# Where raw weights lie, when x is asked for, and how far up the queue a chunk's load stands: three edits at the seam between two layers of a four-layer kernel

## The chip, the cores and the metric

The kernel runs on one core of a Trainium2 chip. A core has five engines that run side by side, each its own list of instructions in order: TensorE (PE) multiplies matrices, VectorE (DVE) and ScalarE (ACT) work element by element, GpSimd (POOL) does too, and SyncE (SP) issues transfers between the chip's memory and the on-chip buffer (SBUF), which 16 DMA engines carry out. The metric is the device time of one execution in microseconds (us), as the median of several runs.

## The reference

The input is `x`, 8 images of 96 channels and 64 x 64 pixels. Four layers follow one another; each adds its result to `x`, and each normalises its input over groups of three channels of one image first:

```
x = x + L0(gn(x))   # a selective state-space scan along all 4096 pixels of an image
x = x + L1(gn(x))   # real FFT -> gated channel mixing -> inverse FFT -> 1x1 projection
                    # -> batch norm over all 8 images -> gelu
x = x + L2(gn(x))   # 3x3 convolution -> offsets -> bilinear sampling -> patches of 4 x 4 pixels
                    # -> four scans (two orders, each forward and backward) -> layer norm -> gate
x = x + L3(gn(x))   # deformable 3x3 convolution
```

Two facts matter here. The batch norm of L1 takes its mean and variance over all eight images, so no image of L1 can be finished until the last has been transformed. And L2 works on chunks of 512 pixels (8 rows of an image), each of which needs normalised `x` with one row above and one below.

## The kernel before

Layer 0 and layer 2, and layer 3 too, are written out by hand as a list of slots: for every slot and engine a list of small functions, issued in that order (`Plan`, `Slots`, and `sl.at(slot, queue, function)`). "sp" stands for the queue of transfers. Layer 1 (the Fourier layer) is written in order of its loops. What is not under such an order is placed by the framework's scheduler, which fills each engine's list by its own estimate of when things are ready.

**Layer 1** goes through the images one after the other: `load` (both halves of `xh`), `down` (L808, into `tr`), `along` (L833, reads `tr`), `gate`, `project`, `back`, `up`, and `store` (L930 to L932), which writes the image `y` to memory in two transfers and reads it back in another layout as `yr`. A tile pool `l1y` has four buffers for `yr`, so the last four images (4 to 7) are still on chip at the end; `kept` holds them. Then come the batch norm's constants (L975 to L983). Then `between()` is called, which for this program is `weights2`: the weights of layer 2. Then the last step of layer 1 for the four kept images (L984 to L997): load `x`, `gelu` of `yb` in place, `x + y`, store, and the statistics that layer 2 needs. The other four images (0 to 3) are finished inside layer 2's slots, in 16 pieces of 96 x 1024 elements (`piece`, L1003 to L1020 and L1653 to L1679): five pieces are asked for in slot -92, five in slot -60, six in slot -46, each piece two loads, and each is stored one slot after its add.

**`weights2`** (L1029) loads raw weights and folds them into the form that layer 2 uses. The folded ones live in a pool `l2c` on the right side of SBUF, that is, at its upper end, and stay for all of layer 2. The raw ones (`l2_wx`, `l2_off1`, `l2_xp`, `l2_dt`, `ds` and small ones) live in a pool `l2t`, which is closed when the folding is done. It takes the default side, the left, directly above `yr`.

**Layer 2** has 64 chunks. Chunk `i` has its base at slot `B = 48 i`; one slot holds one group of scans: a load `dd<-delta` (L319), two exponentials on ACT (L327), a product on POOL (L348), two scans and two products on DVE (L1501, L358), two matmuls. Ahead of the scans of a chunk goes `front` (L1176): `load` of `xl` in slot B - 92 (L1185), `normal` in slot B - 89 (L1190, on ACT, into `pad`), the convolution (L1213) from slot B - 86, offsets, and sampling on POOL up to slot B - 46. Its last part, a copy on ACT (L1329), is in slot B - 44. For chunk 1, `normal` stands in slot -41, and so follows this copy of chunk 0 in ACT's order. Within a slot the order of a queue is the order of the `sl.at` calls; the pieces are placed before the chunks.

**Pools and waits.** A pool takes a stretch of SBUF. When a stretch is used again by a later pool, the later pool's first accesses must wait for the earlier use. The argument `reuse_waits` says how: with `"pool"`, the default, a new pool waits for everything in the pools that lay there; with `"tile"`, each tile waits only for the tiles whose bytes it takes. In the kernel before every pool has the default. In bytes per partition, the pools that matter are laid out so: `l1c` 17,792 to 23,460; `l1w` to 31,076; `l1y` 31,104 to 96,640; `l1i` (all working tiles of the Fourier passes) 96,640 to 224,128; after it `l2t` 96,640 to 120,736 and, once that is closed, `l1j` (three buffers for `x`) 96,640 to 145,792; `l2f` 17,792 to 126,816 and `l2w` 126,816 to 180,064; `l2c` 183,328 to 229,344.

Of the kernel before, what the change touches and what calls it, by code (L numbers as in the profile page):

```python
# [18 lines left out]
CH = 96  # L19
IH = IW = 64  # L20
NP = IH * IW
# [28 lines left out]
new = Names()  # L50
# [432 lines left out]
def replicate(nc, out, w):  # L483

    p = w.shape[0]
    nc.vector.tensor_copy(
        out.rearrange("p s (r n) -> p s r n", r=GC),
        w.rearrange("p (s n) -> p s n", s=2).unsqueeze(2).to_broadcast([p, 2, GC, HS]),
    )
# [276 lines left out]
def layer1(S, src, mid, dst, st_in, st_out, images, finish, between):  # L766
# [3 lines left out]
    tc, nc = S.tc, S.nc  # L770
    with ExitStack() as ctx:
        cp = ctx.enter_context(tc.tile_pool(name="l1c", bufs=1))
        wp = ctx.enter_context(tc.tile_pool(name="l1w", bufs=2))
# [13 lines left out]
        kept = {}  # L787

        with ctx1:
            ip = ctx1.enter_context(tc.tile_pool(name="l1i", bufs=1))  # L790
# [190 lines left out]
        nc.vector.tensor_tensor(mv[:, 0:1], mv[:, 0:1], vec[:, 0:1], ALU.subtract)  # L981
        nc.vector.tensor_tensor(sc[:, 1:2], mv[:, 0:1], sc[:, 0:1], ALU.mult)
        nc.vector.tensor_tensor(sc[:, 1:2], vec[:, 2:3], sc[:, 1:2], ALU.subtract)  # L983
        between()  # L984
        with ExitStack() as ctx2:
            ip = ctx2.enter_context(tc.tile_pool(name="l1j", bufs=3))
            psp = ctx2.enter_context(tc.tile_pool(name="l1g", bufs=2, space=PSUM))

            here = list(kept)[-4:]
            for b in here:  # L990
                yb = kept[b]
                xb = new(ip, [CH, NP], "x2")
                nc.sync.dma_start(xb, src[b])
                finish.gelu(yb)
                nc.vector.tensor_tensor(xb, xb, yb, ALU.add)
                nc.sync.dma_start(dst[b], xb)
                S.image_stats(st_out[:, b, :], xb, wp, psp, "ps")  # L997
# [30 lines left out]
def weights2(S, cp):  # L1028

    tc, nc = S.tc, S.nc  # L1030
    with tc.tile_pool(name="l2s", bufs=4, space=PSUM) as psa:
        ps_of = lambda: new(psa, [128, NW], "ps_s")

        win = S.load("l2_win", cp)
        off2 = S.load("l2_off2", cp)
        vec = S.load("l2_vec", cp)
        wout = S.load("l2_wout", cp)
        kmean = S.load("k_mean", cp)

        sc = new(cp, [HD, 2], "sc")  # L1040
        sh = new(cp, [HD, 2], "sh")
        S.rsqrt(sc, vec[:, :, 4], cp, "bn")
        nc.vector.tensor_tensor(sc, sc, vec[:, :, 1], ALU.mult)
        nc.vector.tensor_tensor(sh, vec[:, :, 0], vec[:, :, 3], ALU.subtract)
        nc.vector.tensor_tensor(sh, sh, sc, ALU.mult)
        nc.vector.tensor_tensor(sh, sh, vec[:, :, 2], ALU.add)

        wds = new(cp, [CH, DI], "wds")

        wg = new(cp, [HD, 2, CH], "wg")  # L1050
        wb = new(cp, [HD, 2, CH], "wb")
        for h in range(2):
            for t, k in ((wg, 5), (wb, 6)):
                nc.vector.tensor_scalar(
                    t[:, h, :], wout[:, h, :], vec[:, h, k : k + 1], None, ALU.mult
                )

        woff = new(cp, [CH, KT, DI], "woff")  # L1060
        rep_w = new(cp, [CH, 4, 2, 2, 128], "rep_w")
        wd = new(cp, [CH + 1, 4, DI], "wd")
        wuu = new(cp, [CH, 2, DI], "wuu")
        nc.vector.tensor_copy(wuu, win[:, :DI].unsqueeze(1).to_broadcast([CH, 2, DI]))

        centre = new(cp, [HD, 2, HD], "centre")
        nc.vector.tensor_tensor(centre[:, 0, :], S.ident[:HD, :HD], kmean, ALU.subtract)
        nc.vector.tensor_scalar(centre[:, 1, :], kmean, -1.0, None, ALU.mult)
        with tc.tile_pool(name="l2t", bufs=1) as tp:
            wx = S.load("l2_wx", tp)  # L1070
            off1 = S.load("l2_off1", tp).rearrange("e h k o -> e h (k o)")
            xp = S.load("l2_xp", tp)
            dtw = S.load("l2_dt", tp)
            ds = new(tp, [CH, 4, DI], "ds")
            nc.sync.dma_start(ds, S.ins["l2_d"].unsqueeze(0).to_broadcast([CH, 4, DI]))
            nc.vector.tensor_tensor(ds[:, 0:2], ds[:, 0:2], ds[:, 2:4], ALU.add)
            nc.vector.tensor_tensor(wds, ds[:, 0], ds[:, 1], ALU.add)
            nc.vector.tensor_tensor(wds, wds, win[:, :DI], ALU.mult)
            flat = woff.rearrange("c k o -> c (k o)")
            for n in range(4):  # L1080
                at = slice(432 * n, 432 * n + 432)
                ps = ps_of()
                for h in range(2):
                    nc.tensor.matmul(
                        ps[:CH, :432], wx[:, h, :], off1[:, h, at], start=h == 0, stop=h == 1
                    )
                nc.scalar.copy(flat[:, at], ps[:CH, :432])
            xpm = new(tp, [CH, 1, 4 * (RK + 2 * NS)], "xpm")
            ps = ps_of()
            for h in range(2):  # L1090
                nc.tensor.matmul(
                    ps[:CH, : 4 * 38],
                    wx[:, h, :],
                    xp[:, h].rearrange("e k c -> e (k c)"),
                    start=h == 0,
                    stop=h == 1,
                )
            nc.vector.tensor_copy(xpm[:, 0, :], ps[:CH, : 4 * 38])
            for k in range(4):
                at = 38 * k + RK  # L1100
                for what in range(2):
                    replicate(
                        nc, rep_w[:, k, what], xpm[:, 0, at + what * NS : at + (what + 1) * NS]
                    )
                ps = ps_of()
                for h in range(2):
                    nc.tensor.matmul(
                        ps[:RK, :CH], xp[:, h, k, :RK], wx[:, h, :], start=h == 0, stop=h == 1
                    )
                low = new(tp, [RK, CH], f"low{k}")  # L1110
                nc.vector.tensor_copy(low, ps[:RK, :CH])
                ps = ps_of()
                nc.tensor.matmul(ps[:CH, :DI], low, dtw[:RK, k, :], start=True, stop=True)
                m = ORDER.index(k)
                nc.vector.tensor_copy(wd[:CH, m, :], ps[:CH, :DI])
                nc.sync.dma_start(wd[CH : CH + 1, m], S.ins["l2_dt"][RK : RK + 1, k])
        return dict(
            win=win, off2=off2, kmean=kmean, sc=sc, sh=sh, wds=wds, wg=wg, wb=wb, woff=woff,
            rep_w=rep_w, wd=wd, wuu=wuu, centre=centre,
        )  # L1120


def layer2(S, src, dst, st_in, st_out, images, cp, W, ready, finish):


    tc, nc = S.tc, S.nc
    with ExitStack() as ctx:
# [8 lines left out]
            )  # L1136
        )

        fp = ctx.enter_context(tc.tile_pool(name="l2f", bufs=1))
        wp = ctx.enter_context(tc.tile_pool(name="l2w", bufs=1))  # L1140
        sl = Slots(S, cp, wp, psd)
        log_exp_tables(S)
        acol = sl.negative_exp("l2_alog")
# [33 lines left out]
        def front(ch, b, pad, xs, c, B):  # L1177
# [4 lines left out]
            def load():  # L1182
                ch["x"] = new(fp, [CH, 10 * IW], "xl", bufs=2)
                r = 8 * c - 1
                nc.sync.dma_start(  # L1185
                    ch["x"][:, : (hi - lo) * IW], src[b][:, (r + lo) * IW : (r + hi) * IW]
                )
# [11 lines left out]
                r = 0 if c == 0 else 9  # L1199
                nc.gpsimd.memset(pad[:, r, :], 0.0)  # L1200

            sl.at(B - 92, "sp", load)
            sl.at(B - 89, "act", normal)
            if c in (0, NC - 1):
                sl.at(B - 89, "pool", border)
# [102 lines left out]
            def between():  # L1308
                nc.gpsimd.tensor_tensor(ch["bot"], ch["bot"], ch["top"], ALU.subtract)
# [384 lines left out]
        for n, b in enumerate(images):  # L1694
            im = {"bns": new(fp, [CH, NC, 6], f"bns{n % 2}")}
            for c in range(NC):
                i, ch = NC * n + c, {}
                B, pad, xs = PER * i, pads[i % 4], samples[i % 2]
# [388 lines left out]
def program(tc, ins, out, images=range(NB), layers=(0, 1, 2, 3)):  # L2087
    images = list(images)
    with ExitStack() as ctx:
# [9 lines left out]
        def weights():  # L2099
            cp = ctx2.enter_context(tc.tile_pool(name="l2c", bufs=1, side="right"))  # L2100
            held.extend((cp, weights2(S, cp)))

        for n, layer in enumerate(layers):
            to = last if n == len(layers) - 1 else scratch(f"x{layer + 1}_", [CH, NP])
            if n == 0 and layer:
                first_stats(S, x0, st[layer], images)
            if layer == 0:
                layer0(S, x0, to, st[0], st[1], images)
            elif layer == 1:
                mid = scratch("y_", [CH, NP])  # L2110
                finish = Finish(S, x0, mid, to, new(S.pool, [CH, 2], "bn_sc"))
                images, ready = layer1(
                    S, x0, mid, to, st[1], st[2], images, finish, weights if 2 in layers else lambda: 0
                )
            elif layer == 2:
                if not held:
                    weights()
                layer2(
                    S, x0, to, st[2], st[3], images, *held, len(images) if n == 0 else ready, finish
                )  # L2120
                ctx2.close()
            else:
                layer3(S, x0, scratch("t_", [NP - IW, 2, CH]), to, st[3], images)
            x0 = to
# [26 lines left out]
```

## Time and profile before

| what | value |
|---|---|
| time, median of 3 runs | 17438.37 us (17433.97 to 17443.99) |
| the profiled execution | 18287.47 us, its span 18285.7 us |
| DVE busy | 16268.6 us (89% of the span) |
| POOL busy | 15303.1 us (84%) |
| PE busy | 14310.8 us (78%), at a granted clock of 0.900 |
| ACT busy | 10307.5 us (56%) |
| transfers | 2689.99 MB, 147 GB/s over the span |
| layer 1's first load; layer 2's first `xl`; layer 3's first load | at 3021.4, 3803.2 and 14482.5 us |

The profile is one execution, recorded instruction by instruction. "SPq" marks the issue of a transfer on the queue of SP; when its data has landed is read from the waits of those who use it. A line such as "A <- B: 102.6, 2, 75.7" says that A waited for B 102.6 us in all, 2 times, 75.7 us at most. In the chain of waits each line is a start, a length and what ran, and each follows from the one above it.

### The profile page before, as it was taken

The page shows a single profiled execution, that of the slowest core. Times are in us where ns is not written, and L with a number is a line of the kernel's source. Part 1 is how long each engine was busy: PE and PEld are TensorE (multiplying, and loading weights), DVE is VectorE, ACT ScalarE, POOL GpSimd, SP SyncE. Part 2 cuts the span into 40 slices and gives each one's busy share as a digit, 9 for nine tenths or more (in the row PEclk, how much of TensorE's full clock was granted, in tenths as well). Part 3 has the DMA queues.
Part 4 walks back from the last instruction along what each step waited for, and adds up shares of the span by engine and source line. Part 5 has one row for each costly group of instructions (what it writes and reads, how often), then busy time and mean ns, then how long its engine had stood idle before and what let it go on. Part 6 is the DMA issues. An engine that isn't in the chain of part 4 may idle for free.

```text
span 18285.7 us, 141860 instructions
## 1 busy us (share of the span) xinstructions
PE 14310.8 (78%) x34756; PEld 5304.7 (29%) x34756; DVE 16268.6 (89%) x16810; ACT 10307.5 (56%) x17016; POOL 15303.1 (84%) x9100
## 2 busy tenths in 40 slices
PE   8999998858888888898898988889888644434333
PEld 2323334723333333333333333333333211111111
DVE  7999997559999999999999999999999766767667
ACT  6777775546666666766666666676666411111100
POOL 7999995049999999999999999999999656656555
PEclk8999998879999999999999999999999866666666
DMA  7888886269999999999999999999999745444444
GB/s 128 151 153 151 151 151 107 56 139 157 158 158 158 158 158 157 159 157 158 158 157 159 157 159 158 158 158 158 158 157 158 139 127 152 143 136 144 135 129 120
DMA packets 941060, 2689.99 MB, mean 147 GB/s; under 512 B 274482, under 2 KB 276223, under 8 KB 938605
## 3 DMA queue, kind: packets, MB, share of 16 engines
q1 hardware_dynamic: 792781, 2227.79, 70.0%
q0 software_dynamic: 147456, 453.13, 8.4%
q8 instruction: 284, 4.65, 0.1%
q14 instruction: 539, 4.42, 0.1%
HBM read 579.53 MB, written 87.69 MB: 36 GB/s over the span
## 4 chain that ended last, share of the span: by engine, by line
POOL 21%; PE 21%; issue 20%; DVE 18%; another core or an unknown queue 11%; ACT 5%; DMA 4%; SPq 0%; POOLq 0%; DVEq 0%; ACTq 0%
POOL dbu L348 12%; PE ps_y L366 9%; DVE ps_d L1501 7%; DVE dbu L358 6%; DMA dd<-delta 3%; POOL dbu L353 2%; PE ps_k L577 2%; PE ps_a L1820 2%; POOL sp_m L1435 1%; POOL delta L1443 1%; PE ps_o L2054 1%; DVE ps_d L675 1%; POOL sp_w L1438 1%; PE ps_k L1213 1%
## 5 line engine op out<-in xcount | busy, mean ns | idle before, releaser
L348 POOL TENSOR_TENSOR dbu<-dd,brep 128x1024 f32<-128x1024 f32 x3840 | 9062.4, 2376 | 187.8 <-DMA dd<-delta 127.2
L366 PE MATMUL ps_y<-dbu,k_red 128*96 128x512 f32 x15360 | 7447.2, 612 | 817.3 <-DVE dbu L358 496.5
L1501 DVE TENSOR_TENSOR_SCAN ps_d<-ps_d,dbu 128x512 f32<-128x512 f32 x5760 | 6710.3, 1208 | 83.7 <-POOL dbu L348 68.9
L327 ACT ACTIVATE ps_d<-dd,l_alog 128x512 f32<-128x512 f32 x7680 | 4991.7, 681 | 2708.3 <-DVE dbu L358 2571.5
L358 DVE TENSOR_TENSOR dbu<-ps_d,crep 128x512 f32<-128x512 f32 x7040 | 4437.1, 668 | 0.0
L366 PEld LDWEIGHTS ps_y<-dbu,k_red 128*96 128x96 f32 x15360 | 2407.3, 166 | 5459.1 <-issue 3158.6
L1985 POOL DMA_INDIRECT v<-t,idx x2304 | 2185.7, 949 | 1570.1 <-DVE s L2012 730.7
L2012 DVE TENSOR_REDUCE s<-v 128x864 f32<-128x3456 f32 x256 | 1554.2, 6071 | 369.7 <-remote 314.9
L2003 DVE TENSOR_TENSOR v<-v,ps_w 128x3456 f32<-128x3456 f32 x256 | 958.4, 3744 | 735.3 <-ACT ps_w L1995 658.4
L675 DVE TENSOR_TENSOR_SCAN ps_d<-ps_d,carry,dbu 128x512 f32<-128x512 f32 x1120 | 1373.4, 1271 | 80.9 <-POOL dbu L348 50.5
L2031 ACT COPY smp<-ps_t 128x768 f32<-128x768 f32 (+1 forms) x512 | 244.4, 529 | 1793.3 <-remote 1197.4
L1213 PE MATMUL ps_k<-pad,woff 96*96 96x512 f32 x2304 | 1093.8, 597 | 69.4 <-ACT pad L1190 66.9
L1480 PE MATMUL ps_a<-xs,rep_w 96*128 96x512 f32 x2048 | 1097.9, 617 | 53.3 <-ACT brep L1488 51.9
L2023 PE MATMUL ps_t<-k_ident,s 128*128 128x128 f32 (+1 forms) x1792 | 328.3, 334 | 1014.8 <-issue 695.1
L353 POOL TENSOR_TENSOR dbu<-h,crep 128x1024 f32<-128x1024 f32 x320 | 755.7, 2362 | 126.1 <-DVE h L1501 126.1
L1820 PE MATMUL ps_a<-xpad,l_om 96*27 96x512 f32 x1152 | 594.7, 667 | 22.5 <-issue 22.5
L1837 PE MATMUL ps_u<-k_ident,oc 27*128 27x27 f32 x256 | 33.0, 252 | 740.0 <-ACT oc L1832 666.8
L2023 PEld LDWEIGHTS ps_t<-k_ident,s 128*128 128x128 f32 (+1 forms) x1792 | 251.6, 170 | 1149.0 <-issue 985.1
L1213 PEld LDWEIGHTS ps_k<-pad,woff 96*96 96x96 f32 x2304 | 372.1, 164 | 708.9 <-issue 583.1
L1162 POOL MEMSET pad<- 96x660 f32 x4 | 2.4, 648 | 683.1 <-DMA y<-yb 683.1
L1435 POOL TENSOR_TENSOR sp_m<-sp_m,sp_s 128x512 f32<-128x512 f32 x384 | 495.4, 1290 | 59.1 <-ACT sp_s L1423 59.1
L1480 PEld LDWEIGHTS ps_a<-xs,rep_w 96*128 96x128 f32 x2048 | 347.1, 189 | 665.0 <-ACT brep L1488 286.2
(268 smaller groups left out, 17180.5 us busy)
## 6 DMA issues: line engine op xcount, KB each, us to landing
dd<-delta SPq DMA_DIRECT2D x3840, 512.0 KB
v<-t,idx POOLq DMA_INDIRECT x2304
xo<-x SPq DMA_DIRECT2D x128, 192.0 KB
x<-xo SPq DMA_DIRECT2D x128, 192.0 KB
xn<-x SPq DMA_DIRECT2D x64, 192.0 KB
xh<-x SPq DMA_DIRECT2D x16, 768.0 KB
y<-yb SPq DMA_DIRECT2D x16, 768.0 KB
yr<-y SPq DMA_DIRECT2D x8, 1536.0 KB
```

Of the source, the lines that this page charges most:

```text
L327: nc.scalar.activation(da, g.dd[:, 0, :], AF.Exp, scale=g.a[:, i : i + 1])
L348: nc.gpsimd.tensor_tensor(g.dbu, g.dd[:, 1:2, :].to_broadcast([128, 2, NW]), g.b(), ALU.mult)
L353: nc.gpsimd.tensor_tensor(g.dbu, g.both, g.c(), ALU.mult)
L358: nc.vector.tensor_tensor(g.dbu[:, i, :], g.h[i], g.c()[:, i, :], ALU.mult)
L366: self.S.nc.tensor.matmul(y, self.red[:, 80 - GC * g.n : 176 - GC * g.n], g.dbu[:, i, :], start=first and i == 0, stop=last and i == 1,)
L675: nc.vector.tensor_tensor_scan(out, da, dbu, carry[:, n + i : n + i + 1] if c else 0.0, ALU.mult, ALU.add)
L1213: nc.tensor.matmul(ch["pk"][:HD, :], woff[:, k, m * HD : (m + 1) * HD], pad[:, dy : dy + 8, dx : dx + IW], start=k == 0, stop=k == KT - 1,)
L1480: nc.tensor.matmul(dr["pa"], rep_w[:, k, what, s, :], xs[:CH, k % 2, :], start=True, stop=True,)
L1501: nc.vector.tensor_tensor_scan(out[:, way], da[:, way], dbu[:, way], 0.0, ALU.mult, ALU.add)
L1820: nc.tensor.matmul(im["pa"][: 3 * KT, :], om[:, k, :], xpad[:, 8 * c + dy : 8 * c + dy + 8, dx : dx + IW], start=k == 0, stop=k == KT - 1,)
L1985: nc.gpsimd.indirect_dma_start(out=st["v"][:, k].rearrange("p q c -> p (q c)"), out_offset=None, in_=flat, in_offset=bass.IndirectOffsetOn ...
L2012: nc.vector.tensor_reduce(st["s"], st["v"].rearrange("p k q c -> p k c q"), mybir.AxisListType.X, ALU.add,)
```

## The change

There are four edits.

1. The last step of layer 1 opens its pool `l1j` before `between()` instead of after it, issues the loads of `x` of the first three kept images there, and then calls `between()`. Only the fourth image's load stays in the loop. The pool has `reuse_waits="tile"`.
2. The pool `l2t` of the raw weights has `side="right"`: it lies below `l2c`, not above `yr`.
3. The pools `l2f` and `l2w` of layer 2 have `reuse_waits="tile"`.
4. A chunk's load of `xl` stands in slot B - 100 instead of B - 92. `normal` stays in slot B - 89.

```diff
@@ layer1
-        between()
         with ExitStack() as ctx2:
-            ip = ctx2.enter_context(tc.tile_pool(name="l1j", bufs=3))
+            ip = ctx2.enter_context(tc.tile_pool(name="l1j", bufs=3, reuse_waits="tile"))
             psp = ctx2.enter_context(tc.tile_pool(name="l1g", bufs=2, space=PSUM))
 
             here = list(kept)[-4:]
+            x = {}
+
+            def load(b):
+                x[b] = new(ip, [CH, NP], "x2")
+                nc.sync.dma_start(x[b], src[b])
+
+            for b in here[:3]:
+                load(b)
+            between()
             for b in here:
-                yb = kept[b]
-                xb = new(ip, [CH, NP], "x2")
-                nc.sync.dma_start(xb, src[b])
+                if b not in x:
+                    load(b)
+                yb, xb = kept[b], x[b]
                 finish.gelu(yb)
@@ weights2
-        with tc.tile_pool(name="l2t", bufs=1) as tp:
+        with tc.tile_pool(name="l2t", bufs=1, side="right") as tp:
@@ layer2
-        fp = ctx.enter_context(tc.tile_pool(name="l2f", bufs=1))
-        wp = ctx.enter_context(tc.tile_pool(name="l2w", bufs=1))
+        fp = ctx.enter_context(tc.tile_pool(name="l2f", bufs=1, reuse_waits="tile"))
+        wp = ctx.enter_context(tc.tile_pool(name="l2w", bufs=1, reuse_waits="tile"))
@@ front
-            sl.at(B - 92, "sp", load)
+            sl.at(B - 100, "sp", load)
```

## The prediction, made before the kernel was run

> **What bounds the kernel now.** The page comes first: DVE is busy 89% of the span and POOL 84%, but its section of 40 slices shows POOL at 5, 0 and 4 tenths in slices 7 to 9: layer 1, in which POOL has no work, and the seam behind it. The edits act at the seam, so I next cut the time there into stretches. Columns: stretch, its length, then busy time and instructions of each engine, the granted clock, the DMA share, GB/s.
>
> ```profile
> core 0: us, PE busy (x) PEld busy (x) DVE busy (x) ACT busy (x) POOL busy (x), PEclk, DMA share, GB/s
> 3700.00:3746.00 46.00, 14.82 (x44) 6.54 (x44) 14.54 (x51) 18.10 (x10) 5.74 (x9) 0.57 0.61 140
> ...
> 3796.00:3866.00 70.00, 25.97 (x44) 8.39 (x44) 22.98 (x27) 29.86 (x27) 13.21 (x10) 0.62 0.61 161
> 3866.00:3927.00 61.00, 27.68 (x45) 9.24 (x46) 3.51 (x5) 14.23 (x17) 3.27 (x3) 0.64 0.39 95
> ...
> 4100.00:13900.00 9800.00, 8786.98 (x19533) 3096.18 (x19533) 9734.10 (x11247) 6801.38 (x10377) 9592.91 (x5166) 0.99 0.92 158
> ```
>
> From 3700 to 3927 no engine is busy half of the time except DVE in its adds; in the scans after it DVE is busy 99% and POOL 98%. So the seam is bound by latency, and the scans by DVE and POOL. Layer 2 is a fixed order: a seam that ends d earlier ends the kernel d earlier. The chain of waits through the seam:
>
> ```profile
> 3694.17 9.17 DMA y<-yb
> 3703.41 9.23 DMA yr<-y
> 3712.65 7.48 DMA l_xp<-l_xp
> ...
> 3735.81 0.96 PE ps_s L1113 x2
> 3736.79 9.17 DMA x<-x
> ...
> 3746.08 4.43 DVE x L995
> ...
> 3770.36 13.82 DMA x<-x
> ...
> 3788.66 7.05 DMA x<-x
> ...
> 3796.74 6.41 DMA dbu<-y
> ...
> 3803.23 11.77 DMA xl<-x
> ...
> 3815.10 0.88 ACT pad L1190
> ```
>
> `x` is asked for at 3736.79, at once behind the last matmul that reads a raw weight: its buffer is the raw weights' stretch. The pieces' loads wait for the last store of `x` (3788.66 plus 7.05), and chunk 0's `xl` is the eleventh in their queue. Then the timeline of ACT, SP and POOL around chunk 1:
>
> ```profile
> 3864.64 1.11 ACT L1329 COPY xs<-xs 96x512 f32<-96x512 f32 x1 [3.27 <-POOL xs L1316]
> ...
> 3881.31 0.30 SPq L1185 DMA_DIRECT2D xl<-x  x1
> 3892.60 0.92 ACT L1190 ACTIVATE pad<-xl,nm,stats 96x640 f32<-96x640 f32 x1 [26.85 <-DMA xl<-x]
> ...
> 3923.73 3.72 POOL L1435 TENSOR_TENSOR sp_m<-sp_m,sp_s 128x512 f32<-128x512 f32 x3 [59.12 <-ACT sp_s L1423]
> ```
>
> ACT idles 26.85 us for chunk 1's `xl`, issued behind the twelve loads of slot -46; convolution, softplus and POOL hang on it.
>
> **What the Trainium skill says.** "DMA: Bandwidth & Descriptors", section "Queues, rings and completion order": SP has one row of rings, and each DMA engine takes a ring's descriptors in order. The trace agrees: `xl`, 216 KB behind ten loads, took 11.77 us, longer than a 1536 KB load of `x` by itself (9.17). "Perfetto Trace Analysis", section "Per-instruction lifecycle": a DMA's profiled window leaves out the movement of its data. It agrees too: the row above says 0.30 us, the data came 11.29 us later. "SBUF — State Buffer", section "The DMA setup-cost knee", gives about 2 us plus bytes at 436 GB/s, an estimate of 5.6 us for 1536 KB; the trace has 9.17, and I use that. No page bears on how pools wait.
>
> **The change, part by part.**
>
> *Edits 1 and 2, x early.* The new `l1j` is still at 96,640 to 145,792, under `l2t` before; on the right `l2t` takes 24,096 bytes below 183,328, so 159,232 to 183,328, and doesn't touch it. Each `x` tile waits only for `xh` and `tr`. `xh` has been read by 3628.66 (the last copy of its transform into `tr`), `tr` by 3653.1 (its last matmul). So three issues of about 0.4 us and 3 x 9.17 = 27.5 us of transfer, moved past the y stores, the yr load and the weights, can run from 3629 or 3653 on and be over by 3690, where the DMA share is 0.27 (3630 to 3700). That is my choice of place; the trace shows that the scheduler does hoist (a memset of layer 2's constants ran on DVE at 3703.53, ahead of layer 1's last statistics). Behind them on SP stands image 6's y store (3636.30); one load ahead of it costs up to 9 us, and its user, statistics at 3663.63, has about 8 us to spare. The latest place, behind yr and ahead of the weights, is rival 2. Raw weights themselves cost nothing new: same bytes, same order, and still behind the y store, which frees their stretch in both kernels.
>
> The first add then needs only gelu: it starts at 3725.0 (3721.26 plus 3.75) instead of 3746.08, 21 us earlier. What is late next is DVE: weight folding (about 6 us of small DVE work up to 3737) now shares it with the adds, so I take 15 to 21 us. The fourth load keeps its place behind the third store.
>
> *Edit 3, tile waits.* In front of the pieces the wait for the last store goes. Piece buffers `dbu` (126,816 to 151,392) lie over `x` of images 5 and 6, `xl` (18,944 to 24,064) over constants long read. Chunk 0's `xl` then depends on its own image's store alone, a data dependence. Behind the last store's issue this saves 3795.92 - 3788.66 = 7.3 us. The transfer itself still occupies the rings ahead of the loads, so I credit it only in part. If the scheduler also lifts `xl` ahead of that store, it comes as early as 3744, and then the ten pieces' loads (3.84 MB from 3795.92 to about 3815) decide, at about 3783 to 3792.
>
> *Edit 4.* Chunk 0's `xl` moves past ten piece loads; its 216 KB then land about 2 us behind what precedes it, where it took 3815.0 - 3795.9 = 19.1. Chunk 0's `normal`: from 3788.66 take 15 to 21 (adds earlier), then 7 for that store in the rings, 2 to 3 for `xl`: 3777 to 3784, against 3815.1, so 31 to 38 us earlier. The pieces' gelus (3828.72) come 12 us after it, and their loads, landing near 3792, meet that. I take 39, just above the upper end, since a late lift of `xl` by a few us is likely; a full one gives 50.
>
> Chunk 1's `xl` moves from behind the loads of slot -46 to slot -52, behind those of slot -60 and ahead of five stores and twelve loads. Its issue goes from 3881.3 to about 3849 on the old clock, and it lands near 3861, before the copy that ends at 3865.75. The wait of 26.85 us goes whole. What is late next: the third pieces' gelu at 3926.57 would stand at 3899.7; its loads landed by 3892.6 at the latest, so not that. POOL (59.12 us idle) and DVE only wait for ACT there and follow.
>
> For the other 62 chunks `xl` (240 KB) moves past eight `dd` loads on SP, to just behind the store of slot 43; the same bytes in the same 48 slots. POOL waits for `dd` only 57.1 us in all between 4050 and 13900. By the trace's issues and landings, `dd` of the groups right behind that slot lands 4.1 us or more before POOL takes it; 240 KB at 158 GB/s is 1.6 us. Cost 0, hidden under that lead; without it, 62 x 1.6 = 99 us.
>
> **Sum**, on the profiled execution's own time: 18287.5 - 39 - 26.9 = 18221.6, 66 us less. The runs' median is 849 us (4.6%) below the profiled execution, and I can't say in which stage; the same 66 us, taken at face value, give 17438.4 - 66 = 17372.
>
> **Rivals.**
>
> 1. *Lifted:* the scheduler moves `xl` and pieces ahead of the last `x` store, 50 + 27 = 77 or somewhat more, to 95: 17343 to 17361. For it: a border memset of layer 2's slots ran on POOL at 3708.14, ahead of earlier work. Against: SP's order follows the scheduler's own estimate of landings.
>
> 2. *x in the way:* SP's order puts the three loads between yr and the weights. 27.5 us of transfer then delay weights, which DVE's folding and ACT's copies stand behind; also SP held `l_xp` until 3712.65, when yr had landed, so few transfers may be outstanding. The adds start near 3746 as before; left are the load order (27) and 7 to 15: 17438 - 38 = 17400.
>
> 3. *Hidden anyway:* the seam is refilled by pieces. If their loads or adds end last in both gaps, one of the two gains goes: gain 10 to 35, 17415.
>
> 4. *Slower:* the chunk's load behind the store of slot 43 makes `dd` late in each of 62 chunks. It must eat the lead of 4.1 us and then 66/62 = 1.1 us more per chunk before the sign turns, 5.2 us where the transfer is worth 1.6. At 2 us per chunk late: 124 - 66, so 17496.
>
> That `reuse_waits` does nothing on chip would show as rival 3: the data path of edit 4 stands without it.
>
> **How the numbers follow.** My forecast (gain 50 to 76) 0.62; rival 1 0.12; rival 2 0.12 (three quarters of it beyond the bound below); rival 3 0.08; rival 4 0.06. 0.2% of 17438 is 35 us, about what a measurement of this kernel can tell from no change. Faster: 0.62 + 0.12 + 0.09 = 0.83; within: 0.03 + 0.08 = 0.11; slower 0.06. The likeliest's own range is 17362 to 17388. For 8 in 10 I need also most of rivals 1 and 2: 17346 to 17405.
>
> **What would show it.** Right: `x` rows of slots 1 to 3 issued before 3694; the first add at about 3725 to 3731; `normal` of chunk 0 near 3780 and no long wait for `xl` in front of chunk 1's; POOL's 59 us wait on softplus at about 32; the stretch of scans unchanged. Wrong: `l_xp` landing 20 us or more behind yr (rival 2); ACT waiting for piece loads instead of `xl` (rival 3); POOL's wait for `dd` growing from 57 to over 100 us (rival 4).

## The result, and the profile after

The changed kernel takes 17384.11 us (median of 8 runs, 17376.68 to 17395.98), the kernel before, run beside it, 17439.53 us (8 runs, 17433.97 to 17444.63). The ratio is 0.9968, 95% interval 0.9957 to 0.9979: 55 us less (37 to 75). The forecast was 17372, range 17346 to 17405.

The profiled execution of after has a span of 17394.2 us. It can't be set against the first profile of before (18285.7) as a whole; a second profile of before has a span of 17441.2. Of the 844 us between these two, 839 lie in layer 3: behind the last `dd` load it takes 3854.7 us in the first and 3015.9 in the second, and the seam and the scans agree within 2.5 us each. Below, "before" at the seam is the first profile, "before, again" the second.

The same view as before, stretches of time (columns: stretch, length, busy time and instructions of each engine, granted clock, DMA share, GB/s), for the kernel after. Its scans start 63 us earlier, so the later stretches are cut shorter:

```profile
core 0: us, PE busy (x) PEld busy (x) DVE busy (x) ACT busy (x) POOL busy (x), PEclk, DMA share, GB/s
3700.00:3746.00 46.00, 1.26 (x4) 0.85 (x5) 25.16 (x47) 16.16 (x5) 5.65 (x9) 0.51 0.94 217
3746.00:3796.00 50.00, 26.88 (x76) 12.28 (x74) 30.00 (x66) 3.85 (x7) 3.33 (x5) 0.63 0.81 234
3796.00:3866.00 70.00, 40.29 (x68) 12.98 (x69) 26.32 (x30) 41.58 (x42) 13.99 (x10) 0.71 0.70 185
3866.00:3905.00 39.00, 22.40 (x33) 7.27 (x32) 22.81 (x23) 25.84 (x36) 26.34 (x19) 0.57 0.51 103
4041.00:13841.00 9800.00, 8794.89 (x19527) 3102.43 (x19526) 9732.77 (x11244) 6800.62 (x10374) 9593.15 (x5164) 0.99 0.92 158
```

Before, the first stretch had a DMA share of 0.61 and 140 GB/s; now it has 0.94 and 217. The loads of `x` run there beside yr and the weights, and the seam's first 100 us are close to being bound by transfers. The row of the scans is the old one, DVE 9733 us and POOL 9593 us of 9800.

The chain of waits through the seam, kernel after (start, length, what ran):

```profile
3697.57 9.17 DMA y<-yb
3706.80 9.52 DMA yr<-y
...
3724.52 3.81 ACT yr L1023
3728.35 1.80 DVE x L1003
...
3749.15 4.33 DVE x L1003
...
3753.89 15.63 DMA x<-x
3769.61 4.43 DVE x L1003
...
3774.43 0.42 SPq L1193
```

The first add follows gelu at once (3724.52 + 3.81 = 3728.33). Neither raw weights nor the first loads of `x` stand in the chain any longer. What is late next is the fourth load of `x`: it stands behind the third store in SP's order, which is issued when the third add has ended, and takes 15.63 us. Then `xl` is issued 0.4 us behind the last store of `x`, which is the issue at 3774.43. Behind it this view puts loads of the pieces into the chain; ACT's timeline, next, shows otherwise.

ACT's timeline at chunks 0 and 1, kernel after (the bracket is idle time before and what ended it):

```profile
3784.49 0.87 ACT L1198 ACTIVATE pad<-xl,nm,stats 96x576 f32<-96x576 f32 x1 [14.27 <-DMA xl<-x]
3795.36 0.77 ACT L1235 ACTIVATE off<-ps_k,sh,sc 96x512 f32<-96x512 f32 x1 [10.00 <-PE ps_k L1221]
...
3797.45 5.77 ACT L1023 ACTIVATE dbu<-dbu,bn_sc 96x1024 f32<-96x1024 f32 x5
...
3833.41 1.11 ACT L1337 COPY xs<-xs 96x512 f32<-96x512 f32 x1 [3.29 <-POOL xs L1324]
3834.42 0.92 ACT L1198 ACTIVATE pad<-xl,nm,stats 96x640 f32<-96x640 f32 x1
```

ACT waits for `xl`, then 10 us for PE's convolution, and then goes on to the pieces' gelu (3797.45) with nothing but a table load between, so no load of a piece is late. Chunk 1's `normal` follows the copy without a gap; before, 26.85 us stood there. And the waits of POOL, first at the seam, then in the scans (in all, times, longest):

```profile
POOL sp_m L1443 <- ACT sp_s L1431: 30.3, 1, 30.3
...
POOL dbu L348 <- DMA dd<-delta: 55.2, 99, 1.7
```

The first was 59.12 us. The second was, in the kernel before:

```profile
POOL dbu L348 <- DMA dd<-delta: 57.1, 98, 1.4
```

To compare kernels I take each trace's own time from the issue of the last `y` store (3693.5 on before's clock), which cancels what layers 0 and 1 vary from one execution to the next. In microseconds:

| from the last `y` store's issue to | before | before, again | after |
|---|---|---|---|
| first add of `x` | 52.5 | 52.5 | 31.4 |
| last add of `x` | 90.7 | 90.8 | 72.7 |
| chunk 0's `xl` issued | 109.7 | 110.5 | 77.5 |
| chunk 0's `normal` | 121.6 | 120.7 | 87.6 |
| chunk 1's `xl` issued | 187.8 | 186.5 | 121.7 |
| chunk 1's `normal` | 199.1 | 197.4 | 137.5 |
| first `dd` load: the seam's end | 258.2 | 255.9 | 194.7 |
| first to last `dd` load (the scans) | 10479.3 | 10478.5 | 10483.3 |
| from there to the end (layer 3) | 3854.7 | 3015.9 | 3019.2 |

The seam ends 63.5 us earlier, or 61.2 against the second profile.

### The profile page after: what moved, and what is told of

Read it like the earlier page. It is cut to its first block, busy times and chain, and to the rows that moved or that the text cites. A ratio compares the mean times of both kernels' runs of the same rounds, so it can differ in the third digit from the quotient of the medians.

```text
span 17394.2 us, 141852 instructions
## 1 busy us (share of the span) xinstructions
PE 14384.4 (83%) x34756; PEld 5357.3 (31%) x34756; DVE 16280.9 (94%) x16810; ACT 10314.6 (59%) x17016; POOL 15310.1 (88%) x9100
## 4 chain that ended last, share of the span: by engine, by line
POOL 31%; issue 24%; DVE 19%; PE 18%; DMA 4%; ACT 4%; SPq 0%; POOLq 0%; DVEq 0%; ACTq 0%
POOL v L1993 12%; POOL dbu L348 10%; DVE ps_d L1509 9%; PE ps_y L366 9%; DVE dbu L358 7%; DMA dd<-delta 3%; PE ps_k L577 2%; POOL dbu L353 2%; POOL sp_m L1443 1%; POOL delta L1451 1%; POOL delta L1459 1%; DVE ps_d L675 1%; ACT ps_d L327 1%; POOL sp_w L1446 1%; PE ps_a L621 1%
## 5 line engine op out<-in xcount | busy, mean ns | idle before, releaser
L2020 DVE TENSOR_REDUCE s<-v 128x864 f32<-128x3456 f32 x256 | 1549.4, 6052 | 26.5 <-PE ps_a L1828 0.5
L2031 PE MATMUL ps_t<-k_ident,s 128*128 128x128 f32 (+1 forms) x1792 | 364.4, 367 | 1369.3 <-DVE s L2020 1368.9
L1221 PE MATMUL ps_k<-pad,woff 96*96 96x512 f32 x2304 | 1093.0, 597 | 26.5 <-ACT pad L1198 23.9
L1221 PEld LDWEIGHTS ps_k<-pad,woff 96*96 96x96 f32 x2304 | 371.9, 164 | 665.4 <-issue 582.3
L1443 POOL TENSOR_TENSOR sp_m<-sp_m,sp_s 128x512 f32<-128x512 f32 x384 | 493.1, 1284 | 30.3 <-ACT sp_s L1431 30.3
L577 PE MATMUL ps_k<-xn,wk 96*96 96x512 f32 x1024 | 500.7, 612 | 3.1 <-ACT xn L551 2.4
```

Of the source, the lines that this page charges most:

```text
L1221: nc.tensor.matmul(ch["pk"][:HD, :], woff[:, k, m * HD : (m + 1) * HD], pad[:, dy : dy + 8, dx : dx + IW], start=k == 0, stop=k == KT - 1,)
L2020: nc.vector.tensor_reduce(st["s"], st["v"].rearrange("p k q c -> p k c q"), mybir.AxisListType.X, ALU.add,)
```

## The experiments

My theory: two gains that add up, one for chunk 0 from edits 1 to 4, one for chunk 1 from edit 4. The rivals: one of the two is hidden behind the other; the moved load costs something in the scans; edits 2 and 3 do the work. Differences are against runs of before taken beside each kernel. Their medians are 17437.09 us (edit 4 alone and undone, two chunks, edit 3 undone), 17440.53 (edit 2 undone, the two places of `x`, adds on POOL), 17441.9 (sum in `yr`'s buffer, `xl` on ACT) and 18276.51 (both together). Places in the seam are in us from the issue of the last `y` store, as in the table.

**Edit 4 alone**, put into the kernel before:

```diff
-            sl.at(B - 92, "sp", load)
+            sl.at(B - 100, "sp", load)
```

> The kernel before with only the chunks' loads moved to slot B - 100. If a chunk's load is what holds the seam (my steps for edit 4): chunk 1's wait of 27 us goes, and chunk 0's load leads the pieces' loads instead of following them, which is worth about 15 us until the pieces' own loads decide: about -40 us against the kernel before. If the loads of x are what holds it, and the chunk's load is hidden behind the pieces: -10 us or less.

**Edit 4 undone**, with edits 1 to 3 kept: the same line the other way in the kernel after.

> The changed kernel with the chunks' loads back in slot B - 92, so edits 1 to 3 alone. By my steps the wait for chunk 1's load is back in full (27 us) and chunk 0's load is again the eleventh in its queue (12 us): about -16 us against the kernel before. If the loads of x are what holds the seam: -40 us or more.

Edit 4 alone: 17398.59 us (0.9977, interval 0.9967 to 0.9986), 38.5 less. Edits 1 to 3 alone: 17422.09 (0.9991, 0.9982 to 0.9999), 15.0 less. The sum is 53.5, and both together gave 55.4. Each interval is some 30 us wide, so the runs alone leave room; the seam doesn't: it ends at 213.1 and 238.0, so 42.8 and 17.9 before the second profile's 255.9, together 60.7 of 61.2. They add, and nothing of one hides the other. ACT's timeline of the two kernels, edit 4 alone first:

```profile
3797.65 0.87 ACT L1190 ACTIVATE pad<-xl,nm,stats 96x576 f32<-96x576 f32 x1 [60.27 <-DMA xl<-x]
...
3847.59 0.92 ACT L1190 ACTIVATE pad<-xl,nm,stats 96x640 f32<-96x640 f32 x1
```

```profile
3791.66 0.87 ACT L1198 ACTIVATE pad<-xl,nm,stats 96x576 f32<-96x576 f32 x1 [29.09 <-DMA xl<-x]
...
3869.21 0.92 ACT L1198 ACTIVATE pad<-xl,nm,stats 96x640 f32<-96x640 f32 x1 [26.80 <-DMA xl<-x]
```

With edit 4, chunk 1's wait is gone although `x` is as late as before; without it, 26.80 us stand there although `x` is early. So the second gain belongs to edit 4 alone, and of the first some 15 us do (edit 4 alone brings chunk 0's `normal` from 120.7 to 105.9).

**Does the moved load cost anything in the scans?** The new slot for the first two chunks only:

```diff
-            sl.at(B - 100, "sp", load)
+            sl.at(B - (100 if B < 2 * PER else 92), "sp", load)
```

> The changed kernel with slot B - 100 for chunks 0 and 1 only, B - 92 for the other 62. If the move is free in the stretch of scans: the same time as the changed kernel, about -55 us, within 5. If the earlier load costs each chunk something there (its dd loads land with 2.6 to 3.3 us of lead in the changed kernel where it was 4.1 to 5.8 before): faster than the changed kernel, by 62 times what it costs, say 10 to 60 us more.

17380.56 us (0.9966, 0.9954 to 0.9978), 56.5 less, against 55.4 for the whole change. In the runs the other 62 chunks cost nothing that can be told. The traces show a little: the scans took 10478.5 to 10479.5 us in the four traces with the old slot for these chunks (10479.4 here), and 10479.7 to 10484.5 in the ten with the new slot for all. That is 2 us more on the mean and 6 at most.

**Edit 3 undone**, the waits of `l2f` and `l2w` as before:

```diff
-        fp = ctx.enter_context(tc.tile_pool(name="l2f", bufs=1, reuse_waits="tile"))
-        wp = ctx.enter_context(tc.tile_pool(name="l2w", bufs=1, reuse_waits="tile"))
+        fp = ctx.enter_context(tc.tile_pool(name="l2f", bufs=1))
+        wp = ctx.enter_context(tc.tile_pool(name="l2w", bufs=1))
```

> The changed kernel with the default waits for the pools l2f and l2w, so edit 3 undone. If the wait for the last store of x ends the chain in front of chunk 0's load: 7 us slower than the changed kernel, -48 against the kernel before. If that store's transfer stands ahead of the load in the rings anyway: at most 3 us slower, -52 to -56.

17380.67 us (0.9968, 0.9956 to 0.998), 56.4 less: beside the other edits, edit 3 is worth nothing that the runs can tell. SP's and ACT's timelines of this kernel:

```profile
3770.94 0.33 SPq L1193 DMA_DIRECT2D xl<-x  x1
...
3774.38 0.87 ACT L1198 ACTIVATE pad<-xl,nm,stats 96x576 f32<-96x576 f32 x1 [15.85 <-DMA xl<-x]
```

`xl` is issued 84.5 us from the last `y` store instead of 77.5, because it waits for the last store of `x` to end. But its data is used 3.4 us after its issue, where after needs 10.1 (3784.49 - 3774.43). `normal` comes at 88.0 against 87.6. The 7 us spent waiting for the store before the issue are spent behind the store after it: same queue, same end. The seam ends at 197.6 here and at 194.7 in after; the kernel with two chunks, whose seam has all the edits of after, has 196.9, so traces of one seam differ by 2 us or more, and up to 3 us for edit 3 stay open.

**Edit 2 undone**, the raw weights on the left again (`l1j` is open by then, so they lie above it):

```diff
-        with tc.tile_pool(name="l2t", bufs=1, side="right") as tp:
+        with tc.tile_pool(name="l2t", bufs=1) as tp:
```

> The changed kernel with the raw weights' pool on the left side again, so edit 2 undone: opened after the pool of x, it lies above it (145,792 to 169,888), not over it. By my account of what x waits for, the side is then worth nothing: the changed kernel's time, -55 us against the kernel before, within 4. If the side itself matters: 10 us or more slower than the changed kernel.

17385.73 us (0.9969, 0.9957 to 0.9981), 54.8 less, seam end 194.6. What frees `x` from the weights is that `l1j` is opened first; the side is then worth nothing.

**Where do the loads of `x` stand?** In after the scheduler didn't lift them. SP's timeline of the kernel after:

```profile
3706.80 0.31 SPq L932 DMA_DIRECT2D yr<-y  x1
3707.16 1.43 SPq L993 DMA_DIRECT2D x<-x  x3
...
3730.12 0.31 SPq L194 DMA_DIRECT2D l_off<-l_off  x1
3737.45 0.31 SPq L194 DMA_DIRECT2D l_xp<-l_xp  x1
```

They stand between yr and the weights: the order of rival 2. Two kernels move them. The first has the place of my forecast, ahead of the last image's `y` stores: `yb` gets a pool of its own (`bp`), `l1j` is opened straight behind the Fourier passes, and an order by hand puts three loads ahead of that store. More moves with them: four small weights now stand ahead of yr, and the fourth load of `x` behind the first store of `x` instead of the third.

```diff
+        bp = ctx.enter_context(tc.tile_pool(name="l1b", bufs=1))
...
-                    im["yb"] = new(ip, [128, CH // 2, IW], "yb")
+                    im["yb"] = new(bp, [128, CH // 2, IW], "yb")
...
+        with tc.manual_schedule():
+            for b in here[:3]:
+                load(b)
+            store(ims[-1])
+            stats(ims[-1])
```

> The changed kernel with the three loads of x put by hand ahead of the last image's y store, where I had expected them (the last y image gets a pool of its own for it; the order of SP then also brings four small weights ahead of yr, and the fourth x directly behind the first store of x). If x and weights in each other's way cost something in the changed kernel: -63 us against the kernel before, 8 more, since the fourth load of x then lands before its add. If gelu and the adds on DVE set the end there anyway: -55, within 3. If the early loads hold up the y store: slower than the changed kernel, up to 27 us.

The second goes the other way, weights first:

```diff
+            between()
             for b in here[:3]:
                 load(b)
-            between()
```

> The changed kernel with the weights' loads issued ahead of the three loads of x, which follow at once. If the delay of the weights (about 25 us in the changed kernel) or the late fourth x ends the chain: 5 to 8 us faster than the changed kernel, -60 to -63 against the kernel before. If neither does: -55, within 3. If x behind the weights comes too late for its adds: slower than the changed kernel by up to 8.

Both took 17379.88 and 17379.82 us (0.9965 and 0.9966), 60.7 less each, with intervals of 0.9951 to 0.9979 and 0.9954 to 0.9978: not to be told from after. By the traces the seam ends at 190.6 with `x` issued from 47.6 us ahead of the store, at 194.7 with `x` at 26.5 us behind it, and at 194.7 in after, with 10.2. The first add with weights first comes 9.5 us later than in after (40.9), the last only 0.7 later (73.4), and chunk 0's `normal` at the same 87.5. So with after's `normal` and after's end of the seam, its gain by the runs is 5 us larger: 5 us between two medians is more than these runs can tell, though for weights first that met the faster of my expectations (the other kernel lies between mine).

Why does `x` ahead of the store bring only 4 us? The three early loads bring nothing: the four adds start at 31.4, 46.1, 56.0 and 65.8, where after has 31.4, 35.8, 52.1 and 72.7. Only the last is earlier, and its load is the fourth, issued at 46.2 instead of 57.0. One more kernel takes away the wait of the fourth load for the first store, by adding into `yr`'s buffer instead of `x`'s, on top of the early loads:

```diff
-                nc.vector.tensor_tensor(xb, xb, yb, ALU.add)
-                nc.sync.dma_start(dst[b], xb)
-                S.image_stats(st_out[:, b, :], xb, wp, psp, "ps")
+                nc.vector.tensor_tensor(yb, xb, yb, ALU.add)
+                nc.sync.dma_start(dst[b], yb)
+                S.image_stats(st_out[:, b, :], yb, wp, psp, "ps")
```

> As the kernel with x ahead of the last y store, and x + y is written over y instead of over x, so that the fourth load of x waits for the first add alone and no longer for its store. If the adds on DVE and the transfers behind them decide, as the trace of that kernel says: its time, -61 us against the kernel before, within 4. If the fourth x is still late: 5 or more faster.

17373.32 us (0.9961, 0.9947 to 0.9975), 68.6 less. The median met my other expectation, 5 us or more faster, but the trace doesn't bear it out: the fourth load is issued at 36.5 instead of 46.2, the last add starts at 66.3 instead of 65.8, and the seam ends at 190.3, as without that edit. The stretch of its adds, by the view of stretches:

```profile
3719.00:3760.00 41.00, 13.05 (x49) 6.63 (x47) 38.15 (x58) 15.50 (x10) 1.09 (x2) 0.58 0.50 153
```

DVE is busy 38.15 of 41 us: the adds (4.4 us) and statistics (5.4) of the last three images follow one another on it, 9.8 us apart, and between the first two adds it also folds weights. With `x` there in time the seam's first part is bound by DVE by its busy time, and a fourth load 9.7 us earlier was worth nothing.

**Adds on POOL.** Then two of the four adds could go to POOL, idle there, in the kernel with early `x` and the sum in `x`'s buffer:

```diff
-                nc.vector.tensor_tensor(xb, xb, yb, ALU.add)
+                add = nc.gpsimd if b in here[1:3] else nc.vector
+                add.tensor_tensor(xb, xb, yb, ALU.add)
```

> As the kernel with x ahead of the last y store, and the adds of images 5 and 6 on GpSimd, which is idle there. If DVE's adds and statistics (4 x 9.3 us) then set the end of the seam, two adds off it give up to 8 us more: -66 to -71 against the kernel before. If the transfers (the last store of x, chunk 0's load, the pieces' loads) set it: -60 to -64.

17386.78 us (0.997, 0.9959 to 0.9981), 53.8 less; the seam ends at 199.6, 9 us later than with all adds on DVE (190.6). The timelines of POOL and DVE:

```profile
3716.54 18.29 POOL L1010 TENSOR_TENSOR x<-x,yr 96x4096 f32<-96x4096 f32 x2 [8.18 <-ACT yr L1030]
```

```profile
3712.80 4.42 DVE L1010 TENSOR_TENSOR x<-x,yr 96x4096 f32<-96x4096 f32 x1 [3.01 <-ACT yr L1030]
```

One add takes 9.1 us on POOL and 4.4 on DVE. The second POOL add ends at 3734.83, the third store follows it, and the scheduler put the fourth load behind that store in SP's order, not behind the first as with all adds on DVE. There it still waits, by the trace, for statistics on DVE: its issue moves from 46.2 to 63.2 us, and the last add from 65.8 to 77.2. A miss, and an instructive one: the work left the bound engine, but a load's issue hung on it. What the move would give with the load left in its place wasn't run.

**Before once more, unchanged**, for a profile to set against:

> The kernel before, unchanged, for a second profile: its profiled execution was 849 us longer than its runs, and against the later profiles nearly all of it (3854.7 us where they have 3015 to 3019) lies behind the last load of the scans, in layer 3. If that was this one execution alone: layer 3 near 3016 us, and a span near 17437; from the last y store to the first load of the scans 258 us as in the first profile, or a few less if the profile of the seam was off too, since the runs show 5 to 8 us less gain than the traces of the seam.

Its numbers stand in the table. In the second profile the seam has the old times, and layer 3 has 3015.9 us.

**The load on a queue of its own.** Chunk 0's `xl`, and only that, issued by ACT instead of SP, in the kernel after:

```diff
-                nc.sync.dma_start(
+                (nc.sync if B else nc.scalar).dma_start(
```

> The changed kernel with chunk 0's load issued from ScalarE's queue instead of SP's, so that it doesn't stand behind the last store of x in SP's rings. If the order in the rings is what makes it land 10 us after its issue: it lands 3 to 5 us after, normal comes about 9 us earlier, and the seam ends 3 to 6 us earlier, where the pieces' loads decide: -58 to -61 us against the kernel before. If the load takes its 10 us wherever it stands: -55, within 2.

17375.31 us (0.9964, 0.995 to 0.9978), 66.6 less. ACT's timeline:

```profile
3761.22 0.35 ACTq L1193 DMA_DIRECT2D xl<-x  x1
3764.01 0.87 ACT L1198 ACTIVATE pad<-xl,nm,stats 96x576 f32<-96x576 f32 x1 [2.56 <-DMA xl<-x]
```

`xl` is used 2.8 us after its issue. It also goes out 4.2 us ahead of the last store of `x`, which it had stood behind, so the two effects, another queue and an earlier place, aren't told apart. The place would do: on SP with that store over, edit 3 undone had 3.4 us. `normal` comes at 75.3, 12.3 us earlier than in after, but the pieces' first gelu only 5.1 us earlier (95.4 against 100.5), and the seam ends at 189.6. That is what I expected, but not for the reason that I gave, the pieces' loads. PE's timeline:

```profile
3770.73 0.48 PE L216 MATMUL ps<-gs_mv,k_group 96*96 96x1 f32 x2 [10.71 <-DVE gs_mv L214]
3771.90 0.48 PE L223 MATMUL ps<-gs_v,k_group 96*96 96x1 f32 x2 [0.69 <-DVE gs_v L221]
3772.24 9.74 PE L1221 MATMUL ps_k<-pad,woff 96*96 96x512 f32 x18
```

The convolution (L1221) stands behind the matmuls of the last image's statistics in PE's order, and those wait for DVE; `normal` was done at 3764.88. The first piece's `y` had landed by 3776.9 (SP's issue at 3776.87 had waited for it), and its gelu starts at 3784.11. So the last `x + y` and its statistics are late next.

**Both together**, early `x` with the sum in `yr`'s buffer, and `xl` on ACT:

> The two that were ahead, together: x ahead of the last y store with the sums written over y, and chunk 0's load on ScalarE's queue. If the pieces' loads, which follow the last store of x on SP, then decide: the seam ends 1 to 4 us before that of the first of the two (190.3 us from the last y store), -66 to -72 us against the kernel before. If chunk 0's load decided in that kernel: the seam ends 8 us or more earlier.

18200.94 us against 18276.51 of before beside it (0.9958, 0.9946 to 0.997), 75.6 less. All of these runs, of both kernels, took some 0.84 ms longer, in this trace again in layer 3 (3866.6 us; the scans took 10481.2), so the difference and the ratio are to be read, not the time. The seam ends at 186.8, 3.5 us before the kernel with early `x` and the sum in `yr`'s buffer. ACT's timeline:

```profile
3733.07 0.36 ACTq L1199 DMA_DIRECT2D xl<-x  x1
...
3766.14 0.87 ACT L1204 ACTIVATE pad<-xl,nm,stats 96x576 f32<-96x576 f32 x1 [30.53 <-DVE nm L1164]
```

`xl` is asked for 33 us ahead, and `normal` waits for DVE's last step of the statistics (`nm`): at 76.0 it is no earlier than in the kernel with `xl` on ACT alone (75.3). The seam's end is as I expected, again not for the reason given: chunk 0's load decides nothing any more, and the statistics do. These two kernels with the sum in `yr`'s buffer have the lowest ratios; their intervals overlap with after's, so only the traces put them ahead, by 4 us (early `x`) and 8 us (both) at the seam.

## Why the prediction was right, and where its steps were not

**The sum.** 66 us predicted; the seam gained 61.2 to 63.5 and the runs 55.4, with an interval (37 to 75) that holds all of these. Both gains came the way they were forecast, one from each stretch of waiting, and add; the number is 2.5 to 5 us above the seam's gain and 11 above the runs'. The places and edits that were to make the first gain were in part the wrong ones, as follows.

**Chunk 0, 39 us.** Measured from the table: 34.0 at `normal` (33.1 against the second profile), and so inside the 31 to 38 that the working gave. By its terms: the last add comes 18.0 earlier (15 to 21 predicted); from there to the issue of `xl` 4.8 us instead of 19.0 (the wait for the store and ten issues gone); from issue to use 10.1 (7 for the store in the rings and 2 to 3 for `xl` predicted). The term that failed is the allowance above the upper end, up to 39, for a late lift of `xl`: SP kept `xl` behind the last store of `x`, so rival 1 didn't happen, and 5 us of the forecast with it. An `xl` lifted without the rest could not have brought much more: with it on ACT, 12.3 us at `normal` became 5.1 at the gelu, since the statistics of the last image are late next, which my working had left out. Rival 3's sign, ACT waiting for loads of pieces, did not show in the kernel after.

**Chunk 1, 26.9 us.** Measured: `normal` of chunk 1 is 61.6 us earlier, 34.6 of that was there already when chunk 0's copy on ACT ended, and 27.0 is left (25.6 against the second profile, whose wait for `xl` was 25.53 us). Edit 4 alone and edit 4 undone show the cause. What follows was predicted as well: POOL's wait for softplus near 32 (30.3), and no piece ends later.

**Edit 1, the place of the loads: wrong.** `x` of slots 1 to 3 wasn't issued before 3694 but at 3707.16, in the order of rival 2. Yet the first add came at 3728.35, on before's clock at 3725.0, at the start of the 3725 to 3731 that I had derived from the early place. That is luck in part: even behind yr the first load had landed (3723.3) before gelu ended (3728.33). So the order was rival 2's and its price was not. That rival had two parts. Raw weights do come late: `l_xp` is issued 30.7 us behind yr (3737.45 against 3706.80), where it was 9.2; the last folded offset weight is copied at 58.0 us instead of 40.5. But they have room until the first convolution behind `normal` at 87.6. And the adds don't stand behind the folding: the scheduler put the first add ahead of it on DVE. I had taken "DVE's folding stands behind the weights" for "the adds do". My sign of the rival, "`l_xp` 20 us or more behind yr", came true and told nothing of the time. The place that I had forecast, made by hand, is worth 4 us at the seam's end, and that through the fourth load. Nor do loads of `x` cost 9.17 us each: that is one load from its issue on, with a second issued 0.4 us behind it; in a row they land about every 7 us, so the 27.5 us were some 4 too many (an estimate: 9.2 + 2 x 7).

**Edit 3: credited in part, worth nothing.** The working said itself that the store still occupies the rings; the kernel with the old waits shows that all but 0.4 of the 7.3 us goes there, by the time of `normal`. This is what the Trainium skill states in "DMA: Bandwidth & Descriptors", section "Queues, rings and completion order", that each DMA engine takes a ring's descriptors in order: the trace agrees, with 10.1 us from issue to use right behind the store and 3.4 us when the issue waits until the store is over.

**Edit 4 in the scans: 0 predicted.** POOL's wait for `dd` is 55.2 us (57.1), and restricting the edit to two chunks gains nothing that can be told. The lead did shrink: from landing to POOL's use, `dd` of the three groups behind the new place of the load had 4.1, 4.5 and 5.7 us on the mean and now has 3.3, 2.6 and 2.6. The forecast's "4.1 us or more" was such a mean: in some chunks the lead was 0.1 us, that is, POOL was waiting, before as after. Rival 4 needed 5.2 us of delay per chunk; the lead lost about 1 to 3. It was nearly hidden: 2 us more in 62 chunks, with up to half of the cover gone.

**From 61 to 55.** The profiled execution of after is the slowest of its 8 runs. Against the second profile of before it has 11.8 us more in layer 1 ahead of the last `y` store (680.9 against 669.1 from the layer's first load), 4.8 more in the scans and 3.3 more in layer 3, and 5.8 less in layer 0: 61.2 - 11.8 - 4.8 - 3.3 + 5.8 = 47.1, and the spans differ by 47.0. The layer 1 term is not shown to be the change's: of the seven kernels with this layer 1, four have 669.2 to 670.3 in their profiled execution and three 679.3 to 680.9, and in these three that execution was the slowest of its runs. The scans may have cost up to 5 us (2 on the mean of the traces). What else makes up the difference between 61 and 55 is within the interval and stays open.

**The 849 us of the profiled execution.** I couldn't say in which stage they were; they are in layer 3, and the kernel with both had them in all its runs, as had before beside it. There layer 3 moves 136 to 139 GB/s instead of 176 to 177, at a granted clock of 0.66 to 0.67 instead of 0.71. Why is open; taking the 66 us at face value was right, since the seam is the same in both.

## What to carry to other kernels

When a small load ends a wait, look first at what stands ahead of it in its queue: moving one line of the order was worth 38 us here, and three edits to pools and places 15, two of which could be undone, one at a time, at no cost that shows. A wait taken away in front of an issue brings nothing if the transfer waited for still stands ahead in the same queue. And when a place in an order is predicted, price each user behind it by its own due time: the weights were 20 us late and nobody missed them.

## What the runs showed of the hardware

- SP held back issues until earlier transfers had landed. In after, yr, three loads of `x` and four small ones are issued within 4 us; the next four issues come at 3716.33, 3723.31, 3730.12 and 3737.45: one as yr lands, then one about every 7 us, which is one load of `x` (1536 KB, so some 220 GB/s). In each of these the wait is for the transfer issued eight before it on SP. The first store of `x`, whose add ended at 3732.7, went out at 3744.49, held last by the load of `l_off` eight ahead. What sets the eight wasn't tried. SP's waits from 3690 to 3800:

```profile
SPq L194 <- DMA x<-x: 20.1, 3, 7.0
...
SPq L194 <- DMA yr<-y: 5.8, 1, 5.8
SPq L1004 <- DMA l_off<-l_off: 4.5, 1, 4.5
```

- An f32 add of 96 x 4096 took 9.1 us on POOL and 4.4 on DVE.
- Layer 3, which gathers by index, took 3015 to 3019 us in twelve traces and 3855 and 3867 in two, one of the kernel before and one of the last kernel here. The seam and the scans didn't feel it.
